# The soft-disc layer of a four-layer kernel: the disc projection with its columns as weights, one chain an image, and a new timetable

## The chip, the cores and the metric

The kernel runs on one core of one Trainium2 chip. A core has a matrix engine (TensorE, PE in the profile, with its weight loads shown apart as PEld), a vector engine (VectorE, DVE), an activation engine (ScalarE, ACT), a general engine (GpSimd, POOL) and a queue engine that issues the DMAs (SyncE, SP). Each works through its own list of instructions in order. The matrix engine writes to PSUM, of which this layer uses eight banks, and POOL works on SBUF only. The metric is device time in microseconds: the median of the runs.

## The reference, cut to what matters

Eight images of 32 x 32 tokens with 256 channels go through four layers, each of the form x + layer(groupnorm(x)). The change is in the fourth: attention in 8 heads of 32 over a 7 x 7 window, with a soft disc per token and head that masks the window.

```python
qkv = silu(x @ w_qkv.T);  q, k, v = split(qkv)
q = rope(rms_norm(q, w_qn));  k = rope(rms_norm(k, w_kn))   # over the 32 of a head
wp = silu(x @ w_wp.T + b_wp)                  # 16 columns: a width and a sharpness for each head
width = sigmoid(wp[..., :8]) * max_dist + 0.5
sharp = sigmoid(wp[..., 8:]) * 9.5 + 0.5
soft_mask = sigmoid((width - rel_dist) * sharp)
scores = scores - (1 - soft_mask) * 10000
out = softmax(scores) @ v_window
y = silu((rms_norm(out, w_on) + v) @ w_out.T)
```


Rope turns q and k of one head by the same angles, so it falls out of their product, and the kernel leaves it out. All arithmetic is in float32.

## The kernel before, in words

`layer3` (L2090) goes over 64 groups: 8 images, in each 2 chunks of 4 heads (a chunk J is image J // 2, half J % 2), in each chunk 4 column strips of the image. One group's life is spread over several turns of the main loop over m (the `for m in range(-2, N + 2)` in the printed code). In turn m the loop writes out, in this order, for all engines: the scores of group m + 2 (L1807, PE), the division of group m by its sums (L1843 on DVE, L1846 on POOL), the window mask of group m + 3 (L2241, POOL), the first four exponentials of group m + 1 (L1836, ACT), two of the four logits steps of group m + 2 (L1825, DVE), then fillers, the second four exponentials, the other logits, the turning of group m - 1 (L1858 transposes on PE, L1863 copies on DVE) in two halves, each half followed by fillers and by four tanh of group m + 4 (`soft`, L2234, ACT), then the product with the values of group m - 2 (L1873 PE, L1879 DVE). The order on PE, ACT, DVE and POOL is exactly the order written.

Everything else is a filler with a due time in turns and quarters of a turn: `fill.add(at, unit)`. `units(at)` issues those that are due, at four places in a turn: m after the first exponentials, m + 0.25 after the first half of the turning, m + 0.5 after the second half, m + 0.75 at the end. A unit's PE part, and for a projection also its ACT part, is issued at that place; what follows on DVE and POOL is a closure, and `finish()` runs one step of every open closure, four times a turn: before the fillers of m, after the second exponentials, and after each group of four `soft`.

The fillers of a chunk J, whose first group is n = 4J (`plan_chunk`, L2355): `project(J, s, h)` (L2146), two matmuls of 128 x 512 on the normed image xq, a tanh on ACT (L2143), then on DVE the product (L2168 for q, L2170 for k and v) and on POOL the square (L2178); s is 0 for q, 1 for k, 2 for v, h is the half of the image. `squares_sum` (L2245) sums the squares on PE, `roots` (L2267) takes their roots on ACT with a table load each way, `head_scales` (L2278) spreads them on PE and multiplies k and then q on DVE (L2288); the scores of the chunk wait for that product. `vturn` (L2292) and `keep` (L2298) write v to memory for the windows.

The fillers of an image b, n = 8b (`plan_image`, L2368): statistics, mean and root of the group norm, `normed(b, c)` (L2119, one ACT instruction of 1.23 us for each half of the channels, L418), the disc projection, and the tail of the image before (scale, output projection, store). `discs(b, u)` (L2184) takes four blocks of 128 tokens: for each block and each half of the channels the tokens are the weights and the 16 columns of w_wp, padded to 128, are streamed (L2191). The result lies with tokens on partitions. Then a chain of a bias add on DVE (L2198), tanh on ACT (L2206), a product on DVE (L2211), tanh on ACT (L2216), and three small DVE steps (`scales`, L2223 to L2225). There are two such chains an image. `soft` of the image's first group, in turn n - 4, reads the result.

Big tiles (an image, a normed image, the weights of the layer) come from a pool of three buffers (`K.big`, L168): the weights keep one for the whole layer, so x of an image and xq of an image take the other two, and xq of image b goes where xq of image b - 1 lay. PSUM tiles come from one ring of eight (`st.ring`, L1786).

Of the kernel before, what the change touches and what calls it, by code (L numbers as in the profile page):

```python
# [10 lines left out]
F32 = mybir.dt.float32  # L11
AF = mybir.ActivationFunctionType
ALU = mybir.AluOpType
# [3 lines left out]
P = 128  # L17
# [2072 lines left out]
def layer3(tc, K, src, dst, n_img, a, first):  # L2090
    nc = tc.nc
    with tc.tile_pool(name="l3c", bufs=1, reuse_waits="tile") as cp, tc.tile_pool(
        name="l3w", bufs=1, reuse_waits="tile"
    ) as wk, tc.tile_pool(name="l3p", bufs=1, space=PSUM, reuse_waits="tile") as pp:
        x, xq, vT, disc, xr, fac, sqs, tok = ({} for _ in range(8))

        def load(b):
            x[b] = K.big("x")
# [6 lines left out]
        st = DiscStream(K, wk, cp, pp, n_img, 6)  # L2105
# [40 lines left out]
        def project(J, s, h):  # L2146
            b, c = divmod(J, 2)
            if h == 0:
                if s == 0:
                    st.q[b, c] = wk.tile([P, L], F32, name="qT", bufs=2)  # L2150
                elif s == 1:
                    st.k[b, c] = kpad[J % 2]
                else:
                    vT[b, c] = wk.tile([P, L], F32, name="vT", bufs=5)
            ps = st.ring("qkv_ps")
            for kc in range(2):
                o = s * C + c * P
                nc.tensor.matmul(  # L2158
                    ps, w[:, kc, o : o + P], xq[b][:, kc, h * HALF : (h + 1) * HALF],
                    start=kc == 0, stop=kc == 1,  # L2160
                )
            th = half_silu(ps)

            def rest():
                d = dest(J, s, h)
                if s == 0:
                    q = st.q[b, c][:, h * HALF : (h + 1) * HALF]
                    nc.vector.scalar_tensor_tensor(q, th, 1.0, ps, ALU.add, ALU.mult)  # L2168
                for k in range(2 if s else 0):
                    nc.vector.scalar_tensor_tensor(  # L2170
                        d[:, k], part(th)[:, k], 1.0, part(ps)[:, k], ALU.add, ALU.mult
                    )
                if s == 2:
# [4 lines left out]
                nc.gpsimd.tensor_mul(part(sq), d, d)  # L2178

            return rest  # L2180

        def discs(b, u):  # L2184
            if u == 0:
                disc[b] = wk.tile([P, 8, 16], F32, name="disc", bufs=2)
            ps = st.ring("wp_ps")
            for i in range(4):
                tok = slice((4 * u + i) * P, (4 * u + i + 1) * P)
                for kc in range(2):  # L2190
                    nc.tensor.matmul(  # L2191
                        ps[:, i * P : (i + 1) * P], xq[b][:, kc, tok], w[:, kc, 768:],
                        start=kc == 0, stop=kc == 1,
                    )

            def rest():
                d = disc[b][:, 4 * u : 4 * u + 4, :]
                nc.vector.tensor_add(  # L2198
                    d, ps.rearrange("p (t g) -> p t g", g=P)[:, :, 0:16],
                    bwp.unsqueeze(1).to_broadcast([P, 4, 16]),  # L2200
                )
                return silu

            def silu():
                th = wk.tile([P, 4, 16], F32, name="dth", bufs=2)
                nc.scalar.activation(th, disc[b][:, 4 * u : 4 * u + 4, :], AF.Tanh)  # L2206
                return lambda: silu2(th)

            def silu2(th):
                d = disc[b][:, 4 * u : 4 * u + 4, :]  # L2210
                nc.vector.scalar_tensor_tensor(d, th, 1.0, d, ALU.add, ALU.mult)  # L2211
                return sigmoid

            def sigmoid():
                d = disc[b][:, 4 * u : 4 * u + 4, :]
                nc.scalar.activation(d, d, AF.Tanh, scale=0.5)  # L2216
                return scales

            def scales():
                d = disc[b][:, 4 * u : 4 * u + 4, :]  # L2220
                wd, sp = d[:, :, 0:8], d[:, :, 8:16]
                md = math.sqrt(2.0) * 3
                nc.vector.tensor_scalar(wd, wd, md / 2, md / 2 + 0.5, ALU.mult, ALU.add)  # L2223
                nc.vector.tensor_scalar(sp, sp, 9.5 / 4, 10.5 / 4, ALU.mult, ALU.add)
                nc.vector.scalar_tensor_tensor(wd, wd, -1.0, sp, ALU.mult, ALU.mult)  # L2225

            return rest

# [49 lines left out]
        def head_scales(J, s):  # L2278

            ps = [st.ring("fac_ps") for _ in range(2)]  # L2280
            for h in range(2):
                g = slice(32 * (2 * s + h), 32 * (2 * s + h) + 32)
                nc.tensor.matmul(ps[h], spread[g, s], fac[J][g], start=True, stop=True)

            def rest():
                for h in range(2):
                    d = dest(J, s, h)
                    nc.vector.tensor_mul(d, d, part(ps[h]))  # L2288

            return rest  # L2290
# [62 lines left out]
        fill = Fillers()  # L2353

        def plan_chunk(J):  # L2355

            n = 4 * J
            for i, at in enumerate((-6.75, -6.25, -5.75, -5.25)):
                fill.add(n + at, lambda i=i: project(J, 1 - i // 2, i % 2))
            for h in range(2):  # L2360
                fill.add(n - 5 + h / 4, lambda h=h: project(J, 2, h))
                fill.add(n - 4 + h / 4, lambda h=h: vturn(J, h))
                fill.add(n - 3 + h / 2, lambda h=h: head_scales(J, 1 - h))
            fill.add(n - 3.5, lambda: keep(J))

        def plan_image(b):
            n = 8 * b
            if b:  # L2368
                fill.add(n - 15, lambda: load(b))
                for i in range(4):  # L2370
                    fill.add(
                        n - 13 + i / 2 if b > 1 else -1.5 + i / 4,
                        lambda i=i: gn.stats(b, image_parts(x[b]), i),
                    )
                fill.add(max(n - 10, -0.5), lambda: gn.mean(b, later))
                fill.add(max(n - 9.5, 0.25), lambda: gn.root(b, later))
                for c in range(2):
                    fill.add(n - 8.5 + c if b > 1 else 0.75 + c / 4, lambda c=c: normed(b, c))
                for u in range(2):
                    fill.add(n - 6 + u / 2, lambda u=u: discs(b, u))  # L2380
            for c in range(2):
                fill.add(n + 6.75 + 3.5 * c, lambda c=c: tail_sq(b, c))
            fill.add(n + 12.75, lambda: tail_scale(2 * b + 4, b))


            for i in range(4):
                h, m = divmod(i, 2)
                fill.add(n + (14.5, 15, 15.25, 15.75)[i], lambda h=h, m=m: reload(b, m, h))
                fill.add(n + (15.5, 16.25, 16.5, 16.75)[i], lambda h=h, m=m: output(b, m, h))
# [155 lines left out]
```

## Time and profile before

| | |
|---|---|
| median of 3 runs | 3099.14 us (3091.14 to 3104.78) |
| the profiled execution | 3098.01 us |
| its span, first to last instruction | 3096.2 us |
| mean granted TensorE clock | 0.979 |
| the fourth layer | from about 2374 us (first L2191) to the end, some 720 us |
| one image in the steady part | 81.9 us (the same tanh of L2143 at 2611.78 and at 2693.69) |
| busy in 2600 to 2650 | PE 47.87, ACT 45.19, DVE 46.42, POOL 40.60 of 50 us |
| busy in 2650 to 2700 | PE 47.73, ACT 46.51, DVE 38.93, POOL 46.81 of 50 us |
| L2191, the disc projection on PE | 128 matmuls in the layer, 275 ns each as modelled (each recorded as two) |
| L2158, the other projections on PE | 192 matmuls, 592 ns each as modelled |

A line of the timeline has the start in us, the duration, the engine, the line, the operation with output and inputs, the count of merged instructions, and in brackets how long the engine stood idle before it and who released it. A matmul in float32 is recorded as two passes, so "x4" of L2158 are two matmuls. Matmuls are pipelined, so what a run of them costs is read from the start of one line to the start of the next, not from the durations.

### The profile page before, as it was taken

To read this page: it belongs to the slowest core of one execution; us is meant where nothing else is said; L and a number is where in the kernel's file an instruction comes from. 1 tells how busy PE (TensorE), PEld (TensorE's weight loads), DVE (VectorE), ACT (ScalarE), POOL (GpSimd) and SP (SyncE) were. 2 spreads that over 40 slices of the span, in tenths; PEclk is the share of its full clock that TensorE was granted. 3 is DMA by queue.
4 is the path that set the end of the run, shared out by engine and by line. 5 is a ranking of instruction groups with operands and counts; after the bars stand their busy time and mean duration, and the time that the engine had idled before them with its cause. 6 is when DMAs were issued, how large, how long until landed. Compare 5 with 4: busy or idle time off the path is not lost. (4 is left out here: it accounts for less than half of the span.)

```text
span 3096.2 us, 74829 instructions
## 1 busy us (share of the span) xinstructions
PE 2944.2 (95%) x29224; PEld 1573.7 (51%) x29224; DVE 2172.7 (70%) x5249; ACT 2136.7 (69%) x4833; POOL 1736.8 (56%) x1132
## 2 busy tenths in 40 slices
PE   7999999999999899999999999899998899999997
PEld 3323233232332344477777775666665455555554
DVE  4777777777778567766666665667675688888885
ACT  3667676676677556665555553677676899999994
POOL 4666666666666211144455444434344578888886
PEclk9999999999999999999999999999999899999997
DMA  3000000000001366789888864343443112222221
GB/s 140 12 28 1 28 18 11 28 1 28 21 8 42 105 236 233 262 222 225 216 199 216 213 180 162 103 134 106 137 122 117 52 56 83 82 85 82 70 71 61
DMA packets 246945, 325.07 MB, mean 105 GB/s; under 512 B 16192, under 2 KB 185216, under 8 KB 238272
## 3 DMA queue, kind: packets, MB, share of 16 engines
q1 hardware_dynamic: 240208, 299.92, 32.3%
q10 hardware_dynamic: 6384, 20.37, 1.9%
q8 instruction: 231, 3.78, 0.5%
q14 instruction: 122, 1.00, 0.1%
HBM read 216.70 MB, written 103.53 MB: 103 GB/s over the span
## 5 line engine op out<-in xcount | busy, mean ns | idle before, releaser
L693 DVE TENSOR_TENSOR e<-s,ret 128x1024 f32<-128x1024 f32 x512 | 602.4, 1218 | 175.0 <-PE s L687 172.5
L700 ACT ACTIVATE ea<-e 128x1024 f32<-128x1024 f32 x512 | 535.4, 1055 | 257.1 <-DVE e L693 234.5
L702 POOL TENSOR_TENSOR ea<-ea 128x1024 f32<-128x1024 f32 x128 | 304.0, 2375 | 285.7 <-ACT ea L700 217.7
L687 PE MATMUL s<-qk,qk 32*128 32x512 f32 x2048 | 302.2, 641 | 3.1 <-DVE e L693 1.3
L1705 POOL TENSOR_TENSOR e<-e,su 128x616 f32<-128x616 f32 (+2 forms) x128 | 156.6, 1229 | 263.4 <-DVE su L1704 237.4
L739 PE MATMUL num<-e,v 128*32 128x512 f32 x2048 | 271.3, 595 | 0.0
L1846 POOL TENSOR_TENSOR e<-e,su 128x784 f32<-128x784 f32 x128 | 188.8, 1497 | 84.0 <-DVE su L1843 79.8
L2234 ACT ACTIVATE e<-win,disc 128x196 f32<-128x196 f32 x512 | 235.4, 541 | 0.1
L869 PE MATMUL up_ps<-x,wup 128*128 128x512 f32 x512 | 229.1, 602 | 4.0 <-POOL x L237 3.2
L1836 ACT ACTIVATE e<-e,mx 128x196 f32<-128x196 f32 x512 | 226.8, 449 | 4.2 <-DVE mx L1825 4.2
L1700 ACT ACTIVATE e<-e,mx 128x154 f32<-128x154 f32 (+2 forms) x512 | 211.6, 420 | 4.6 <-DVE mx L1688 4.6
L712 PE MATMUL sm<-ea,ones 128*32 128x512 f32 x1536 | 209.6, 607 | 1.6 <-POOL ea L702 1.6
L1291 POOL TENSOR_TENSOR decayed<-state,rb 128x520 f32<-128x520 f32 x48 | 50.8, 1057 | 274.6 <-DVE state L1321 137.4
L1825 DVE CUSTOM_DVE_ANT_0 e<-s,e 128x196 f32<-128x196 f32 x512 | 153.1, 356 | 73.1 <-PE s L1807 63.1
L896 DVE SCALAR_TENSOR_TENSOR cv<-xm,par,cv 128x512 f32<-128x512 f32 x192 | 144.7, 754 | 80.6 <-ACT cv L891 75.9
L2158 PE MATMUL qkv_ps<-xq,w 128*128 128x512 f32 x384 | 192.0, 627 | 8.1 <-ACT xq L418 6.3
L2241 POOL TENSOR_TENSOR e<-e,win 128x784 f32<-128x784 f32 x128 | 198.8, 1575 | 0.3 <-ACT e L2234 0.3
L687 PEld LDWEIGHTS s<-qk,qk 32*128 32x128 f32 x2048 | 84.6, 183 | 195.6 <-issue 86.8
L1085 ACT ACTIVATE d<-d,cols 128x128 f32<-128x128 f32 x512 | 163.3, 391 | 14.3 <-POOL d L1076 13.7
L1863 DVE COPY pts<-pt 112x512 f32<-112x512 f32 x256 | 163.8, 683 | 1.5 <-PE pt L1858 1.5
L869 PEld LDWEIGHTS up_ps<-x,wup 128*128 128x128 f32 x512 | 95.5, 191 | 117.7 <-issue 106.5
L1076 POOL TENSOR_TENSOR d<-cmask,d 128x1024 f32<-128x1024 f32 x64 | 154.0, 2408 | 0.0
(236 smaller groups left out, 6466.9 us busy)
## 6 DMA issues: line engine op xcount, KB each, us to landing
d<-l1rows SPq DMA_DIRECT2D x64, 512.0 KB
x<-x SPq DMA_DIRECT2D x25, 1024.0 KB
v<-l3v SPq DMA_DIRECT2D x320, 56.0 KB
l1xm<-xm SPq DMA_DIRECT2D x16, 1024.0 KB
l1sz<-sz SPq DMA_DIRECT2D x16, 1024.0 KB
xv<-l1xm SPq DMA_DIRECT2D x32, 512.0 KB
l1xa<-xa SPq DMA_DIRECT2D x16, 1024.0 KB
xa<-l1xa SPq DMA_DIRECT2D x16, 1024.0 KB
```

Source lines behind the costliest of these rows:

```text
L687: nc.tensor.matmul(s[:, j % 2], qk[b, 1, c][g, kb * P : (kb + 1) * P], qk[b, 0, c][g, h * HALF : (h + 1) * HALF], start=True, stop=True,)
L693: nc.vector.tensor_mul(e[n, i], s, m)
L700: nc.scalar.activation(ea[n, i], e[n, i], AF.Abs)
L702: nc.gpsimd.tensor_add(ea[n, i], ea[n, i], ea.pop((n - 1, i)))
L712: nc.tensor.matmul(acc["sm"][g, :], ones, two[j // 2][:, j % 2, :], start=kb == 0 and k == 0, stop=kb == 4 and k == 2,)
L739: nc.tensor.matmul(acc["num"][g, :], v[b][:, kb, vc], e[n, j // 2][:, j % 2, :], start=kb == 0, stop=kb == 7,)
L869: nc.tensor.matmul(ps, wup[:, kc, m * P : (m + 1) * P], seg(s)[:, kc], start=kc == 0, stop=kc == 1,)
L1700: self.nc.scalar.activation(p[:, j], p[:, j], AF.Exp, scale=-1.0, bias=mx[:, i, j : j + 1], accum_out=su[:, j : j + 1],)
L1836: self.nc.scalar.activation(e[:, j], e[:, j], AF.Exp, scale=-1.0, bias=mx[:, g, j : j + 1], accum_out=su[:, g, j : j + 1],)
L2158: nc.tensor.matmul(ps, w[:, kc, o : o + P], xq[b][:, kc, h * HALF : (h + 1) * HALF], start=kc == 0, stop=kc == 1,)
L2234: nc.scalar.activation(e[:, j], win[:, 0], AF.Tanh, scale=disc[b][:, i, 8 + h : 9 + h], bias=disc[b][:, i, h : h + 1],)
L2241: nc.gpsimd.tensor_add(e, e, win[:, 1].unsqueeze(1).to_broadcast([P, 4, NWIN]))
```

## The change

The disc projection is turned round: 32 columns of the weights (16 real, 16 zero) are the weights of four tiles of the matrix engine, 32 columns wide each, and each tile streams a quarter of the image (256 tokens). All four results lie in one PSUM bank, 32 partitions each. DVE copies that bank to SBUF, two transposes turn it back to tokens on partitions, and from there one chain of the same kind runs for the whole image instead of two for half each. The last three steps of the chain (`scales`) go from DVE to POOL. The due times change: the first projection of k and both of q are a quarter of a turn earlier, `head_scales` of k is a quarter later, the root of the group norm a quarter earlier, `normed` half a turn and three quarters earlier, and the disc projection sits at -5.75 and -5.5 instead of -6 and -5.5. In `start()` the disc projection comes alone first, and its turning between the two projections of k.

```diff
-        def discs(b, u):
-            if u == 0:
-                disc[b] = wk.tile([P, 8, 16], F32, name="disc", bufs=2)
+        def discs(b):
             ps = st.ring("wp_ps")
-            for i in range(4):
-                tok = slice((4 * u + i) * P, (4 * u + i + 1) * P)
-                for kc in range(2):
+            for kc in range(2):
+                for i in range(4):
                     nc.tensor.matmul(
-                        ps[:, i * P : (i + 1) * P], xq[b][:, kc, tok], w[:, kc, 768:],
-                        start=kc == 0, stop=kc == 1,
+                        ps[32 * i : 32 * i + 32, 0:256], w[:, kc, 768:800],
+                        xq[b][:, kc, 256 * i : 256 * i + 256],
+                        start=kc == 0, stop=kc == 1, skip_group_check=True,
                     )
             def rest():
+                turned[b] = wk.tile([P, 256], F32, name="dsb")
+                nc.vector.tensor_copy(turned[b], ps[:, 0:256])
+            return rest
+
+        def disc_turns(b):
+            d = disc[b] = wk.tile([P, 8, 16], F32, name="disc", bufs=2)
+            t, ps = turned.pop(b), st.ring("dt")
+            for i in range(2):
+                nc.tensor.transpose(
+                    ps[:, i * P : i * P + P], t[:, i * P : i * P + P], K.ident
+                )
+            def rest():
                 nc.vector.tensor_add(
-                    d, ps.rearrange("p (t g) -> p t g", g=P)[:, :, 0:16],
-                    bwp.unsqueeze(1).to_broadcast([P, 4, 16]),
+                    d.rearrange("p (q t) g -> p t q g", t=2),
+                    ps[:, 0:256].rearrange("p (t q g) -> p t q g", t=2, g=32)[:, :, :, 0:16],
+                    bwp.unsqueeze(1).unsqueeze(1).to_broadcast([P, 2, 4, 16]),
                 )
                 return silu
...
             def scales():
-                nc.vector.tensor_scalar(wd, wd, md / 2, md / 2 + 0.5, ALU.mult, ALU.add)
-                nc.vector.tensor_scalar(sp, sp, 9.5 / 4, 10.5 / 4, ALU.mult, ALU.add)
-                nc.vector.scalar_tensor_tensor(wd, wd, -1.0, sp, ALU.mult, ALU.mult)
+                nc.gpsimd.tensor_scalar(wd, wd, -md / 2, -md / 2 - 0.5, ALU.mult, ALU.add)
+                nc.gpsimd.tensor_scalar(sp, sp, 9.5 / 4, 10.5 / 4, ALU.mult, ALU.add)
+                nc.gpsimd.tensor_mul(wd, wd, sp)
...
-            for i, at in enumerate((-6.75, -6.25, -5.75, -5.25)):
+            for i, at in enumerate((-7, -6.25, -6, -5.5)):
                 fill.add(n + at, lambda i=i: project(J, 1 - i // 2, i % 2))
...
-                fill.add(n - 3 + h / 2, lambda h=h: head_scales(J, 1 - h))
+                fill.add(n - 2.75 + h / 4, lambda h=h: head_scales(J, 1 - h))
...
-                fill.add(max(n - 9.5, 0.25), lambda: gn.root(b, later))
+                fill.add(max(n - 9.75, 0), lambda: gn.root(b, later))
                 for c in range(2):
-                    fill.add(n - 8.5 + c if b > 1 else 0.75 + c / 4, lambda c=c: normed(b, c))
-                for u in range(2):
-                    fill.add(n - 6 + u / 2, lambda u=u: discs(b, u))
+                    fill.add(n - 9 + 0.75 * c if b > 1 else 0.25 + c / 4, lambda c=c: normed(b, c))
+                fill.add(n - 5.75, lambda: discs(b))
+                fill.add(n - 5.5, lambda: disc_turns(b))
...
-            rest = [discs(0, 0), discs(0, 1), project(0, 1, 0)]
-            all_of(rest[0], rest[2])
-            all_of(rest[1], project(0, 1, 1))
+            all_of(discs(0))
+            rest = [project(0, 1, 0), disc_turns(0), project(0, 1, 1)]
+            all_of(*rest)
```

The tanh steps of the chain now work on 128 elements a partition instead of 64, and `d` is the whole tile `disc[b]`.

More of the change, by code (lines that the diff above doesn't have):

```diff
@@ L2094, in layer3 @@
     ) as wk, tc.tile_pool(name="l3p", bufs=1, space=PSUM, reuse_waits="tile") as pp:
-        x, xq, vT, disc, xr, fac, sqs, tok = ({} for _ in range(8))
+        x, xq, vT, disc, xr, fac, sqs, tok, turned = ({} for _ in range(9))
         def load(b):
@@ L2180, in project @@
             return rest
-        def discs(b, u):
-            if u == 0:
-                disc[b] = wk.tile([P, 8, 16], F32, name="disc", bufs=2)
+        def discs(b):
             ps = st.ring("wp_ps")
-            for i in range(4):
-                tok = slice((4 * u + i) * P, (4 * u + i + 1) * P)
-                for kc in range(2):
+            for kc in range(2):
+                for i in range(4):
                     nc.tensor.matmul(
-                        ps[:, i * P : (i + 1) * P], xq[b][:, kc, tok], w[:, kc, 768:],
-                        start=kc == 0, stop=kc == 1,
+                        ps[32 * i : 32 * i + 32, 0:256], w[:, kc, 768:800],
+                        xq[b][:, kc, 256 * i : 256 * i + 256],
+                        start=kc == 0, stop=kc == 1, skip_group_check=True,
                     )
             def rest():
-                d = disc[b][:, 4 * u : 4 * u + 4, :]
+                turned[b] = wk.tile([P, 256], F32, name="dsb")
[9 more added lines that the diff above has]
+            def rest():
                 nc.vector.tensor_add(
-                    d, ps.rearrange("p (t g) -> p t g", g=P)[:, :, 0:16],
-                    bwp.unsqueeze(1).to_broadcast([P, 4, 16]),
+                    d.rearrange("p (q t) g -> p t q g", t=2),
+                    ps[:, 0:256].rearrange("p (t q g) -> p t q g", t=2, g=32)[:, :, :, 0:16],
+                    bwp.unsqueeze(1).unsqueeze(1).to_broadcast([P, 2, 4, 16]),
                 )
@@ L2204, in silu @@
             def silu():
-                th = wk.tile([P, 4, 16], F32, name="dth", bufs=2)
-                nc.scalar.activation(th, disc[b][:, 4 * u : 4 * u + 4, :], AF.Tanh)
+                th = wk.tile([P, 8, 16], F32, name="dth", bufs=2)
+                nc.scalar.activation(th, d, AF.Tanh)
                 return lambda: silu2(th)
             def silu2(th):
-                d = disc[b][:, 4 * u : 4 * u + 4, :]
                 nc.vector.scalar_tensor_tensor(d, th, 1.0, d, ALU.add, ALU.mult)
@@ L2214, in sigmoid @@
             def sigmoid():
-                d = disc[b][:, 4 * u : 4 * u + 4, :]
                 nc.scalar.activation(d, d, AF.Tanh, scale=0.5)
@@ L2219, in scales @@
             def scales():
-                d = disc[b][:, 4 * u : 4 * u + 4, :]
                 wd, sp = d[:, :, 0:8], d[:, :, 8:16]
                 md = math.sqrt(2.0) * 3
-                nc.vector.tensor_scalar(wd, wd, md / 2, md / 2 + 0.5, ALU.mult, ALU.add)
-                nc.vector.tensor_scalar(sp, sp, 9.5 / 4, 10.5 / 4, ALU.mult, ALU.add)
-                nc.vector.scalar_tensor_tensor(wd, wd, -1.0, sp, ALU.mult, ALU.mult)
+                nc.gpsimd.tensor_scalar(wd, wd, -md / 2, -md / 2 - 0.5, ALU.mult, ALU.add)
+                nc.gpsimd.tensor_scalar(sp, sp, 9.5 / 4, 10.5 / 4, ALU.mult, ALU.add)
+                nc.gpsimd.tensor_mul(wd, wd, sp)
             return rest
```

## The prediction

> **What bounds the kernel now.** The change is in the last layer alone, so I read that stretch and no share of the whole span: first the busy time of each engine in stretches of 50 us, then the waits of each engine from 2450 to 3000 us, then the order of time around one disc projection.
>
> The stretches (PE, PEld, DVE, ACT, POOL, granted clock, DMA share, GB/s):
>
> ```profile
> 2600.00:2650.00 50.00, 47.87 (x547) 29.43 (x546) 46.42 (x153) 45.19 (x141) 40.60 (x30) 1.00 0.29 87
> 2650.00:2700.00 50.00, 47.73 (x539) 28.96 (x537) 38.93 (x136) 46.51 (x132) 46.81 (x36) 1.00 0.33 101
> ```
>
> No engine stands out, so waits decide. ACT's, from 2450 to 3000 us:
>
> ```profile
> ACT th L2143 <- PE qkv_ps L2158: 34.2, 42, 3.9
> ACT th L2143 <- PE out_ps L2333: 1.6, 7, 0.2
> ACT th L2143 <- POOL e L2241: 1.6, 2, 0.8
> ACT xq L418 <- DVE gn L231: 0.9, 1, 0.9
> ```
>
> That is its whole list: outside it ACT works without a pause. So ACT sets the pace, and time is lost only where a projection's tanh stands for PE. In the image from 2611.78 to 2693.69 (81.9 us) these stands are 1.30, 1.32 and 0.23 in the even chunk and 0.73, 1.02, 0.38, 0.18 and 0.23 (the last for L2333) in the odd one: 2.85 and 2.54, together 5.39 us. The first two lie at the disc projections, as the timeline shows:
>
> ```profile
> 2606.18 0.93 PE L1807 MATMUL s<-kp,qT 32*64 32x196 f32 x32
> 2607.04 2.05 PE L2191 MATMUL wp_ps<-w,xq 128*128 128x128 f32 x16
> 2609.80 1.88 PE L2158 MATMUL qkv_ps<-xq,w 128*128 128x512 f32 x4
> 2611.78 0.60 ACT L2143 ACTIVATE th<-qkv_ps 128x512 f32<-128x512 f32 x1 [1.30 <-PE qkv_ps L2158]
> 2612.39 1.95 PE L2191 MATMUL wp_ps<-w,xq 128*128 128x128 f32 x16
> 2615.29 1.98 PE L2158 MATMUL qkv_ps<-xq,w 128*128 128x512 f32 x4
> 2617.37 0.60 ACT L2143 ACTIVATE th<-qkv_ps 128x512 f32<-128x512 f32 x1 [1.32 <-PE qkv_ps L2158]
> ```
>
> Each disc block holds PE 1.9 us (2607.04 to 2608.93), and after each the tanh of q is late.
>
> **PE, part by part.** Removed: two blocks of 1.88, 3.76 us an image. Added: eight matmuls of 256 columns on 32-column tiles. The nearest row is `squares_sum`, L2253: four matmuls of 512 in four such tiles start at 2707.36 and the next line at 2708.22, 0.86 us. Ours have the same columns for each tile, so 0.86. Going into and out of narrow tiles costs something: L1873's 448 columns a tile would last 448 x 1.68 ns = 0.75 (1.68 from L2253's 0.86 / 512), and it takes 1.02 from start to start, so 0.27. The two transposes: four of L1888 take 0.49 (2710.93 to 2711.42), so 0.25. Sum 1.38; PE gains 2.4 us an image (bounds 2.1 if the transposes pay 0.27 too, 2.65 if tiles switch free).
>
> The Trainium skill, "TensorEngine Tiling (Array Packing)", section Key Properties, speaks against this: a change of tiling mode drains the engine. It gives no duration, and the new order puts one narrow stint between full-width transposes that had none; by the rule the cost is one drain in and one out, which the trace's 0.27 for L1873 would already hold.
>
> **ACT.** Four small tanh become two of twice the width. In place such a tanh takes 0.15 (2614.04 to the `soft` at 2614.19); two of up to 0.21 leave a gain of 0.17 an image (bounds 0.1 and 0.3).
>
> **DVE and POOL of the chain.** DVE loses ten steps an image and gets a copy (0.41, L1879's row), an add (0.22 to 0.41) and one product (0.22 alone, 1.96 at worst in L2211's row, when POOL works on SBUF): 40.7 us over 15 chains become about 10. DVE is not waited for there, since ACT waits for PE only, so I cost it at nothing. POOL's three steps of 64 elements: from 1.04 (512 elements) and 1.50 (784) the slope is 1.7 ns an element and the rest 0.17, so 0.27 each; L224's 0.71 for two elements is the other end; 0.8 to 2.1 in all. The cover is POOL's wait here, with `soft` of the next image on ACT only at 2634.52:
>
> ```profile
> 2622.60 1.03 POOL L2178 TENSOR_TENSOR sq<-qT 128x512 f32<-128x512 f32 x1
> 2630.48 2.95 POOL L1846 TENSOR_TENSOR e<-e,su 128x784 f32<-128x784 f32 x2 [6.84 <-DVE su L1843]
> ```
>
> Without that cover they would cost ACT up to 2.1 us an image.
>
> **The new due times, even chunk.** Here a gain is given back. k's first tanh moves ahead of four exponentials (0.44 each from start to start): ACT is free of the tanh of 2598.34 at 2598.82, does four exponentials, reaches it at 2600.6 and ends at 2601.1, and DVE, whose next closure is its product, stands from 2599.6 (before, it scaled k there). DVE is full from there on: product 0.66, logits 1.13, copies 1.2, k scale 1.2, copies 1.2, q scale 1.2 end at 2607.7 instead of 2606.13. The scores wait for the q scale, so they end at 2608.56 and q's first projection (1.72 + 0.15 to its tanh) at 2610.4. ACT comes at 2608.9 (four exponentials, eight `soft` of 0.46, k's second tanh of 0.5 and four exponentials after 2601.1) and stands 1.6 us where it stood 1.30. Then PE is early: turning 0.87, discs 1.13, turning 0.87, q's second half 1.72 end at 2615.0, ACT comes at 2614.7 and stands 0.25 instead of 1.32; v's second wait of 0.23 goes. Stands 1.85 instead of 2.85, a gain of 1.0 (bounds: 2.85 if q's scale is not late, minus 0.5 if DVE slips another 1.5).
>
> **Odd chunk.** The same move without a disc projection taken out. k's first tanh no longer stands (PE's part is done at 2638.9, ACT comes at 2639.8), its second stands 0.7 instead of 1.02: ACT, earlier by the lost wait and the tanh it has done, comes at 2645.8, and PE, which needs a PSUM bank that DVE's second copy of the turning frees, has it ready at 2646.5. But q's scale ends at 2648.15 as before, the scores at 2648.55, and q's first projection at 2650.6, while ACT, now coming before its four exponentials, is there at 2648.8: 1.85 us where it had none. New too: `normed` moves to n - 9, between the v projections of the image before, whose xq lies in the buffer that it writes. It must wait for the second v projection, a half turning (0.87) and a projection (1.72) behind the first on PE: about 1.0 us, and behind it stand four exponentials, whose sums POOL divides. The waits of 0.38, 0.18 and 0.23 go. Sum 0.7 + 1.85 + 1.0 = 3.55 against 2.54: a loss of 1.0 (bounds: gain 0.5, loss 2.5). Elsewhere: PE waits up to 3.4 us, 19.3 us in seven places, for the square of q before `squares_sum`; q's second half now comes earlier and POOL squares it ahead of the division. That goes, but ACT has no wait behind it, so it is worth nothing. `head_scales` of k moves one `finish` later on DVE; q's, for which the scores wait, stays.
>
> **The start.** Image 0: the first tanh of L2143 (2379.94) comes 2.7 us sooner, but the first `soft` waits for the chain, which now ends on POOL behind memsets that last to 2381.35, two squares (2.1) and its own 0.8 to 2.1: 2384.3 to 2385.6 against 2384.07; I take 0.5 us lost. Image 1: PE waits for xq.
>
> ```profile
> 2433.36 2.08 PE L2158 MATMUL qkv_ps<-xq,w 128*128 128x512 f32 x2 [5.53 <-ACT xq L418]
> 2438.37 0.60 ACT L2143 ACTIVATE th<-qkv_ps 128x512 f32<-128x512 f32 x1 [0.40 <-PE qkv_ps L2158]
> 2445.68 0.60 ACT L2143 ACTIVATE th<-qkv_ps 128x512 f32<-128x512 f32 x1 [3.19 <-PE qkv_ps L2158]
> ```
>
> `normed` moves from 0.75 and 1.0 to 0.25 and 0.5, so xq is complete 3.5 us sooner, and the stands of 0.40 and 3.19 go: 3.6 (bounds 0 and 3.6). Together 3.1 gained.
>
> **Sum.** Seven even chunks at -1.0, seven odd at +1.0, seven times -0.17, start -3.1: -4.3 us. The profiled execution took 3098.0 (span 3096.2 and 1.8 around it), so 3093.7; the median of the runs lies 1.1 above it. I predict 3094, with a range of its own of 3086 to 3103.
>
> **Rivals.** *PE's time arrives in full.* If q's scale is not late, and q's tanh finds its projection ready, seven images save the even chunk's 2.85 + 0.17 and the odd one stays as it was: 21 us, with the start 24, 3074. For it: the two largest stands are at the blocks that shrink. Against: PE waits for DVE's scale at 2606.18, and making the block behind it shorter doesn't move that. *The tanh ahead of the exponentials holds ACT.* At both chunks' first q projection ACT now comes 1.77 us (four exponentials) sooner than PE can serve it. If DVE's q scale slips by 1.5 us more than I have, each of 14 places costs 1.5 more: 21 us, 3115. It turns the gain into a loss from 0.3 us a place on (4.3 / 14), and makes the kernel slower by over 0.5% from 1.5. For it: DVE was full before both places, and its small steps last up to 1.6 us beside POOL. Against: its PSUM-reading copies and scales keep their 0.68 all through. *The change doesn't do what it says:* the four tiles run one after the other, 3.4 instead of 0.86, q's second tanh is 2.6 late again: 7 x 2.3 more, 3110. L2253's row speaks against it.
>
> **How the numbers follow.** What a measurement of this kernel can tell from no change is about 0.5%, 15.5 us. Forecast 0.60, PE's time in full 0.24, ACT held 0.12, tiles in sequence 0.04 (within 0.5% as well). So faster 0.24, same 0.64, slower 0.12. The range takes most of both rivals: 3075 to 3112.
>
> **What would show it.** L2191 gone, eight matmuls in about 0.9 us and a stint of about 1.1 to the next line; ACT's stands at 1.6 and 0.25 in the even chunk, 0.7 and 1.85 in the odd one, and L418 standing about 1.0 for PE; no wait of L2253 for POOL; the 3.19 at the start gone; an image of 81.7 us. Wrong would be: ACT waiting for POOL at the first `soft` of an image, or an image below 80.5 or above 83.

## The result, and the profile after

The changed kernel takes 3115.59 us (median of 12 runs, 3111.74 to 3120.15); beside it the kernel before took 3102.19 us (12 runs). The ratio is 1.0046, with a 95% interval of 1.0034 to 1.0058: the change costs some 14 us. The prediction was 3094, and its range ended at 3112. The profiled execution after took 3111.74 us, with a span of 3109.7 us, and its mean granted clock is 0.973 (before 3096.2 and 0.979).

The time went into the steady part of the fourth layer. From the division of the first image's first group (L1843 on DVE) to that of the last image's it is 575.1 us before and 593.2 after, so 2.6 us an image are lost in the mean, and 3.3 in an undisturbed one (85.2 against 81.9).

In the changed kernel's lines L2188 is the disc projection, L2204 its turning, L2222 the product of its chain, L2226 the second tanh of its chain, L2232 to L2234 its scales on POOL, L2243 `soft`, L2262 `squares_sum`, L2283 `roots`, L2292 and L2297 the two halves of `head_scales` (PE, DVE), L2331 the scale of the tail, L2349 the product behind the output projection. L2143, L2158, L2170, L418, L1807, L1836, L1858 and L1873 are as before.

The stretches of 50 us after (PE, PEld, DVE, ACT, POOL, granted clock, DMA share, GB/s):

```profile
2600.00:2650.00 50.00, 44.85 (x518) 25.81 (x522) 44.70 (x146) 47.95 (x143) 43.02 (x34) 0.99 0.27 81
2650.00:2700.00 50.00, 47.40 (x483) 26.48 (x474) 35.87 (x129) 42.82 (x123) 41.37 (x31) 0.94 0.32 99
```

ACT's waits after, from 2450 to 3000 us (us in total, times, longest); this is the whole list:

```profile
ACT th L2143 <- PE qkv_ps L2158: 49.7, 33, 4.1
ACT xq L418 <- PE qkv_ps L2158: 10.3, 6, 1.7
```

The first line was 34.2 before, in 42 places; now it is fewer places and longer ones. The second line is new. So the frame of the prediction holds: ACT still sets the pace and loses time only to late projections. What is new on the other engines is who waits for k. DVE's and then PE's waits after, in the same stretch:

```profile
DVE kp L2170 <- ACT th L2143: 23.2, 13, 5.9
```

```profile
PE pt L1858 <- DVE kp L2170: 20.4, 13, 5.5
```

Before, the second was not there, and the first was short:

```profile
DVE kp L2170 <- ACT th L2143: 3.8, 2, 3.2
```

Around one such place, an odd chunk's turn n - 7, the timeline of the changed kernel reads:

```profile
2724.61 1.98 PE L2158 MATMUL qkv_ps<-xq,w 128*128 128x512 f32 x4
...
2729.23 0.57 ACT L2143 ACTIVATE th<-qkv_ps 128x512 f32<-128x512 f32 x1
2729.83 0.75 DVE L2170 SCALAR_TENSOR_TENSOR kp<-th,qkv_ps 128x256 f32<-128x256 f32 x2 [0.89 <-ACT th L2143]
2730.73 0.78 PE L1858 MATMUL pt<-idg,e 128*112 128x128 f32 x4 [1.08 <-DVE kp L2170]
2731.44 2.46 PE L2292 MATMUL fac_ps<-fac,spread 32*128 32x512 f32 x4
2732.83 1.28 DVE L2297 TENSOR_TENSOR kp<-kp,fac_ps 128x512 f32<-128x512 f32 x2
2733.83 1.94 PE L1873 MATMUL o<-pts,v 112*32 112x128 f32 x40
2735.70 3.05 PE L2158 MATMUL qkv_ps<-xq,w 128*128 128x512 f32 x4
2738.79 0.60 ACT L2143 ACTIVATE th<-qkv_ps 128x512 f32<-128x512 f32 x1 [3.69 <-PE qkv_ps L2158]
```

k's first projection is done on PE early, but ACT comes to its tanh only behind four exponentials. DVE's next step is the product of that tanh, so DVE stands 0.89 us; PE's transposes write to PSUM alone, and the last four of the turn stand 1.08 us. They go on 0.15 us behind the end of that product (2729.83 and 0.75), as in all 13 places, and 2.1 us ahead of the scale of k (L2297, 2732.83). Now the durations: the spreading for q takes 2.46 us where that for k, at 2727.40, takes 1.41, the values 1.94 instead of 1.09, and k's second projection 3.05 instead of 1.98. The granted clock (the column behind POOL) in windows of 4 us says why:

```profile
2726.00:2730.00 4.00, 3.46 (x18) 1.91 (x16) 3.11 (x9) 4.00 (x14) 4.00 (x4) 1.00 0.33 96
2730.00:2734.00 4.00, 3.27 (x12) 1.47 (x16) 4.00 (x14) 4.00 (x14) 4.00 (x4) 0.63 0.04 11
2734.00:2738.00 4.00, 4.00 (x43) 2.60 (x40) 2.94 (x7) 1.10 (x3) 4.00 (x4) 0.51 0.05 16
```

PE works at half speed for about 7 us after the pause (3.4 us of clock are lost in the last two windows), and ACT, with 1.10 us of work in the last window, waits for it. I read the clock of every run from 2450 to 3000 us in windows of 2 us, counted the stretches of windows below 0.9, and added up (1 - clock) x 2 us: before 5 stretches and 10.2 us, after 12 stretches and 34.1 us.

### The profile page after: what moved, and what is told of

The parts are those of the page before. It is cut to its first block, busy times and chain, and to the rows that moved or that the text cites. A ratio compares the mean times of both kernels' runs of the same rounds, so it can differ in the third digit from the quotient of the medians.

```text
span 3109.7 us, 74566 instructions
## 1 busy us (share of the span) xinstructions
PE 2941.5 (95%) x29112; PEld 1555.5 (50%) x29112; DVE 2150.6 (69%) x5193; ACT 2132.5 (69%) x4817; POOL 1743.7 (56%) x1156
## 3 DMA queue, kind: packets, MB, share of 16 engines
q8 instruction: 231, 3.78, 0.5%
## 5 line engine op out<-in xcount | busy, mean ns | idle before, releaser
L2243 ACT ACTIVATE e<-win,disc 128x196 f32<-128x196 f32 x512 | 236.1, 541 | 2.9 <-POOL disc L2234 2.8
L1836 ACT ACTIVATE e<-e,mx 128x196 f32<-128x196 f32 x512 | 226.9, 448 | 4.2 <-DVE mx L1825 4.2
L2158 PE MATMUL qkv_ps<-xq,w 128*128 128x512 f32 x384 | 204.1, 660 | 5.8 <-ACT xq L418 5.3
L1858 PE MATMUL pt<-idg,e 128*112 128x128 f32 x1024 | 142.1, 281 | 31.1 <-DVE kp L2170 20.4
L1858 PEld LDWEIGHTS pt<-idg,e 128*112 128x112 f32 x1024 | 117.5, 138 | 86.0 <-issue 44.3
```

The lines of the kernel that those rows point to most:

```text
L1836: self.nc.scalar.activation(e[:, j], e[:, j], AF.Exp, scale=-1.0, bias=mx[:, g, j : j + 1], accum_out=su[:, g, j : j + 1],)
L1858: self.nc.tensor.transpose(d[:, g, k], self.tile(n)[:, g, j, k * self.PART : (k + 1) * self.PART], self.K.ident,)
L2158: nc.tensor.matmul(ps, w[:, kc, o : o + P], xq[b][:, kc, h * HALF : (h + 1) * HALF], start=kc == 0, stop=kc == 1,)
L2243: nc.scalar.activation(e[:, j], win[:, 0], AF.Tanh, scale=disc[b][:, i, 8 + h : 9 + h], bias=disc[b][:, i, h : h + 1],)
```

## The experiments

Each kernel was compared with the kernel before on the same chip; ratios carry a 95% interval. Two theories stood at the start: that the new place of k's `head_scales`, on DVE behind k's first product, is the loss (with the fallen clock as what carries it, or with the waits alone), and that `normed`, which now waits for its buffer, is.

**The two halves of the change.** The disc form with all old due times (against the changed kernel):

```diff
-            for i, at in enumerate((-7, -6.25, -6, -5.5)):
+            for i, at in enumerate((-6.75, -6.25, -5.75, -5.25)):
-                fill.add(n - 2.75 + h / 4, lambda h=h: head_scales(J, 1 - h))
+                fill.add(n - 3 + h / 2, lambda h=h: head_scales(J, 1 - h))
-                fill.add(max(n - 9.75, 0), lambda: gn.root(b, later))
+                fill.add(max(n - 9.5, 0.25), lambda: gn.root(b, later))
-                    fill.add(n - 9 + 0.75 * c if b > 1 else 0.25 + c / 4, lambda c=c: normed(b, c))
+                    fill.add(n - 8.5 + c if b > 1 else 0.75 + c / 4, lambda c=c: normed(b, c))
```

> The new form of the disc projection with all due times of the chunks and of the group norm as they were before (the projection at -5.75, its turning at -5.5). Theory 1, k's first projection a quarter earlier holds a PSUM bank in the turn where the scale of k now comes late, PE stands for banks, and its clock falls to half for k's second projection: none of that here, no half-speed k projection, ACT's stands at the q projections shrink to under 0.5 each; 8 to 20 us faster than before. Theory 2, the normalised image waits 1.72 us for its buffer, six times: also gone here, as fast as in theory 1. Theory 3, the disc chain itself costs (its three steps on POOL, the copy, the tiles): as slow as the changed kernel, about 3115.

Measured: 3082.1 us, ratio 0.9949 (0.993 to 0.9967). And the same four lines the other way round, the old disc projection with the new due times:

> The old disc projection, both halves at -6 and -5.5, with the new due times of the chunks and of the group norm. Theory 1 (banks and half clock in the turn of k's first projection): slower than the changed kernel's 1.0046, because the 2.4 us of PE an image are not saved either: 1.006 to 1.012 of before, with k's second projection at half speed in most chunks. Theory 3 (the disc chain costs): within 0.2% of before.

Measured: 3124.99 us, ratio 1.0078 (1.006 to 1.0096). So the disc form gains some 16 us by itself, and the timetable is the whole loss. ACT's list for the old form at the new times has the same 49.7 and 10.3 as the changed kernel's, and 2.3 more. The path is not the same, though: there PE waits for kp 7.2 us in 3 places only, and the clock loses 20.5 us in 10 stretches. What the new times cost the old form besides was not followed.

**Which due time.** First the times of the chunk put back and those of the norm left new (the first two pairs of the diff above):

> The changed kernel with the due times of projections and head scales as before, and the group norm's new ones kept. Theory 1: ACT's stands at k's second projection (2.5 and 3.7 us) go, but L418 still stands about 1.7 for the buffer six times: 5 to 10 us slower than the disc form with all old times, 0 to 12 us faster than before. Theory 2 (the buffer wait alone made the change slower): still 10 us slower than before.

Measured: 3102.92 us, 1.0009 (0.9997 to 1.0021). Against the disc form alone only the norm's times differ, so these cost 0.6% in that company. Then the reverse, `normed` alone put back for the images after the second:

```diff
-                    fill.add(n - 9 + 0.75 * c if b > 1 else 0.25 + c / 4, lambda c=c: normed(b, c))
+                    fill.add(n - 8.5 + c if b > 1 else 0.25 + c / 4, lambda c=c: normed(b, c))
```

> The changed kernel with normed back at -8.5 and -7.5 for images 2 to 7. Theory 2 (buffer wait): 10 us faster than the changed kernel, that is about as before, 3102 to 3106. Theory 1 (banks and half clock): the wait of L418 goes but the stands at k's second projection stay at 2.5 to 3.7; gains at most 1.7 x 6 = 10 us, less where the time turns up at the next stand for PE: 3105 to 3112.

Measured: 3119.54 us, 1.0063 (1.0044 to 1.0083). The 10.3 us of L418 are gone from ACT's list, and yet nothing is gained: the stands at L2158 rise to 53.9, and the clock falls in 15 stretches. The wait for the buffer by itself is not the cause.

**PE kept busy, first attempt.** The spreading matmuls of `head_scales` issued three times:

```diff
-                nc.tensor.matmul(ps[h], spread[g, s], fac[J][g], start=True, stop=True)
+                for _ in range(3 if J else 1):
+                    nc.tensor.matmul(ps[h], spread[g, s], fac[J][g], start=True, stop=True)
```

> The changed kernel with each matmul of head_scales issued three times into the same PSUM bank (the same result, some 3.4 us more work for PE a chunk, placed where PE stands for banks). Theory 1a, half of ACT's stand at k's second projection is the clock, which falls to half because PE pauses in the turn before: the k projection runs at 1.7 instead of 3.0 us, the stands of 2.5 to 3.9 us shrink by about 2 at some 14 places, and the kernel with more work is 10 to 25 us faster than the changed one, 3090 to 3106. Theory 1b, only the waits for banks count and the clock follows from the delay: no gain, or up to 10 us slower than the changed kernel, 3115 to 3125.

Measured: 3177.17 us, 1.0233 (1.02 to 1.0267). PE's wait for kp fell from 20.4 to 4.2 us, but ACT's stands rose to 91.7: the added matmuls stand ahead of k's second projection and of the scales themselves, so they lengthen the path. Inconclusive on the clock, which still fell in 9 stretches.

**k's scale, and its order against k's first projection.** Only `head_scales` put back:

```diff
-                fill.add(n - 2.75 + h / 4, lambda h=h: head_scales(J, 1 - h))
+                fill.add(n - 3 + h / 2, lambda h=h: head_scales(J, 1 - h))
```

> The changed kernel with head_scales back at -3 and -2.5 alone; k's first projection stays at -7, so that both fall into one place, the scale first. Theory 1 (DVE stands for k's first tanh with the scale of k behind it): DVE scales k before it stands, the banks come free sooner, the stands at k's second projection shrink below 2 in the even chunk; 5 to 15 us faster than the changed kernel. If the place of head_scales is without effect: 3115.

Measured (e6 below): 3089.96 us, 0.9958 (0.9945 to 0.9971), and PE's wait for kp at the turning is gone. This one quarter of a turn is worth 0.9%, some 27 us, for q's `head_scales` is at -2.5 in both. Only k's first projection put back, which then follows k's `head_scales` at the same place:

```diff
-            for i, at in enumerate((-7, -6.25, -6, -5.5)):
+            for i, at in enumerate((-6.75, -6.25, -6, -5.5)):
```

> The changed kernel with k's first projection back at -6.75 alone, head_scales of k at the same place ahead of it. Theory 1 (k's first projection is what starts the stands): no half-speed k projection, stands at k's second projection under 1; with the buffer wait of L418 still there 3100 to 3106, near the run with all chunk times back. Rival (q's tanh ahead of the exponentials is what costs): stays at about 3115.

Measured: 3097.37 us, 0.9981 (0.997 to 0.9991): a little below the 3100 to 3106 of Theory 1, and not the rival's 3115. Then the order alone, against the kernel of the scale put back:

```diff
-            for i, at in enumerate((-7, -6.25, -6, -5.5)):
+            for i, at in enumerate((-7.01, -6.25, -6, -5.5)):
```

> The kernel of e6 (k's `head_scales` at -3, ratio 0.9958), with the first projection of k a hundredth of a turn sooner: both are issued at the same place of the turn as there, but the projection comes first, so that its product stands ahead of the scale of k on DVE. Nothing else differs. Theory 1 (the scale stands on DVE behind a product that waits for ACT's tanh, and holds its PSUM banks as long): most of the loss of the changed kernel comes back, 3105 to 3118 (ratio 1.000 to 1.006), with PE waiting for banks in the turning and k's second projection late for ACT. Rival (what costs is only that `head_scales` is issued a quarter of a turn later): as e6, 3085 to 3095.

Measured (e10 below): 3110.49 us, 1.0022 (1.0009 to 1.0034). Both units are issued at the same place of the turn, and swapping them brings back 20 of the 27 us, with the wait:

```profile
PE pt L1858 <- DVE kp L2170: 20.0, 12, 6.0
```

So most of the loss is the order of the two units and not the quarter of a turn. The time is that of Theory 1; its reason, that the scale standing behind the product holds PE, is not what the trace shows. The place from above reads in this run:

```profile
2729.73 0.76 DVE L2170 SCALAR_TENSOR_TENSOR kp<-th,qkv_ps 128x256 f32<-128x256 f32 x2 [0.89 <-ACT th L2143]
2730.40 1.28 DVE L2297 TENSOR_TENSOR kp<-kp,fac_ps 128x512 f32<-128x512 f32 x2
2730.63 0.62 PE L1858 MATMUL pt<-idg,e 128*112 128x128 f32 x4 [1.09 <-DVE kp L2170]
```

PE goes on behind the product, when the scale has only begun. In the kernel with the scale first, all the transposes of that turn run without a wait, and most of them before the product starts:

```profile
2720.15 2.20 PE L1858 MATMUL pt<-idg,e 128*112 128x128 f32 x16
2722.16 0.74 DVE L2170 SCALAR_TENSOR_TENSOR kp<-th,qkv_ps 128x256 f32<-128x256 f32 x2
```

So the order decides whether the transposes wait for k's product at all. It may decide which unit's PSUM bank comes round to them; no run reads the banks, so that is not shown. Next the changed kernel with k's first projection sooner still, so that its tanh is done when DVE comes:

```diff
-            for i, at in enumerate((-7, -6.25, -6, -5.5)):
+            for i, at in enumerate((-7.25, -6.25, -6, -5.5)):
```

> The changed kernel with the first projection of k a quarter of a turn sooner still, at -7.25, ahead of the divisions and of the first four exponentials; k's `head_scales` stays late at -2.75. Theory 1 (DVE's queue: the product of k stands for its tanh and the scale of k behind it): the tanh is done before DVE's product comes, the scale is not held, the banks come free; ratio near e6's, 0.994 to 0.999, and PE's wait for kp at the turning (24 us in 550) falls under 8. Rival (a late `head_scales` costs by itself, since PE's spreading matmuls and the scale then fall into the turning whatever stands ahead of them): 1.002 to 1.007.

Measured (e11 below): 3116.7 us, 1.0047 (1.0031 to 1.0063). Half a miss: PE's wait for kp fell from 20.4 to 5.4 us, as expected, and the time stayed, as did ACT's stands (58.1 us in all, 60.0 in the changed kernel). Its windows around ACT's longest stand (6.64 us, ending at 2662.80) show what took its place:

```profile
2648.00:2652.00 4.00, 3.34 (x45) 2.01 (x44) 3.75 (x17) 4.00 (x17) 2.63 (x2) 1.00 0.31 87
2652.00:2656.00 4.00, 3.82 (x12) 2.03 (x12) 4.00 (x14) 4.00 (x12) 4.00 (x4) 0.53 0.20 57
2656.00:2660.00 4.00, 4.00 (x45) 2.10 (x42) 4.00 (x8) 0.15 (x1) 4.00 (x4) 0.50 0.00 0
```

Two pauses of 0.31 and 0.35 us in the turning, and the clock is at half for the next 8 us all the same. It fell in 10 stretches here, three of them at a wait that is new: PE stands 4.1 us for the second tanh of the disc chain (L2226). That asked for a test of the clock that leaves the path alone.

**The pause filled.** The changed kernel with the four transposes ahead of PE's wait written three times into the same bank, which DVE reads only after that wait; 14 places:

```diff
-        for g in range(2):
+        for _ in range(3 if j == 2 and n % 4 == 0 and n < 56 else 1):
+            for g in range(2):
```

> The changed kernel, with the four transposes ahead of PE's wait for the product of k (L1858, the second half of the turning in the turn of k's first projection) written three times into the same bank: eight transposes more, about 0.87 us of work, in a place where PE stands 0.95 to 1.08 us for a bank anyway, and where DVE reads the result only after that wait. 14 places. The waits, the order and all due times stay. Theory C (the granted clock falls to half because of this pause, and the half clock makes the second projection of k late): PE's wait there shrinks to 0.1 to 0.3, the clock stays at 1.00 in most of those places (12 stretches below 0.9 between 2450 and 3000 us become 3 to 6), the second projection of k takes 1.9 to 2.0 instead of 2.9 to 3.1, ACT's stands for L2158 fall from 49.7 to 25 to 38, and the kernel takes 3093 to 3107. Rival (the wait for the bank is the whole cost and the clock only follows): stands and time as in the changed kernel, 3112 to 3122. Second rival (other pauses take the clock down as well, as in e5): the clock's stretches stay at 9 to 12 and the time within 6 us of the changed kernel.

Measured: 3099.64 us, 1.0003 (0.9989 to 1.0017): 112 transposes whose results nobody needs make the changed kernel 0.4% faster. The same place in its timeline (all lines behind L1853 are one higher here):

```profile
2728.89 1.52 PE L1859 MATMUL pt<-idg,e 128*112 128x128 f32 x12 [0.20 <-DVE oT L2332]
2730.62 0.62 PE L1859 MATMUL pt<-idg,e 128*112 128x128 f32 x4 [0.21 <-DVE kp L2171]
2731.18 1.65 PE L2293 MATMUL fac_ps<-fac,spread 32*128 32x512 f32 x4
2732.77 1.09 PE L1874 MATMUL o<-pts,v 112*32 112x128 f32 x40
2733.78 1.98 PE L2159 MATMUL qkv_ps<-xq,w 128*128 128x512 f32 x4
...
2735.81 0.60 ACT L2144 ACTIVATE th<-qkv_ps 128x512 f32<-128x512 f32 x1 [0.81 <-PE qkv_ps L2159]
```

and its windows:

```profile
2726.00:2730.00 4.00, 3.80 (x24) 2.50 (x23) 3.11 (x7) 4.00 (x15) 4.00 (x4) 1.00 0.32 88
2730.00:2734.00 4.00, 3.79 (x53) 2.30 (x52) 4.00 (x15) 4.00 (x14) 4.00 (x4) 1.00 0.06 18
2734.00:2738.00 4.00, 3.93 (x39) 1.71 (x39) 3.89 (x13) 3.19 (x12) 4.00 (x4) 1.00 0.18 54
```

DVE's wait for the tanh is as long as ever (23.1 us in all), and PE's transposes go on at the same moment (6.12 us behind the start of k's first projection in both), but the clock stays at 1.00 and ACT's stand shrinks from 3.69 to 0.81 us. At this place the wait itself costs little, and the half clock behind it 2.9 us. Over the whole kernel, filling the pauses gives back 0.43%, about half of the 0.88% that putting `head_scales` back gives; what the other half is was not separated. In the even chunks the clock still falls (4 of the 6 stretches left), behind another pause, of 1.43 us, that was not filled.

**Towards a better kernel.** The disc form with the old due times, and its projection a quarter of a turn sooner:

```diff
-                fill.add(n - 5.75, lambda: discs(b))
+                fill.add(n - 6, lambda: discs(b))
```

> The disc form with all old times, and the disc matmuls at -6 instead of -5.75, so that the turning does not stand for DVE's copy (0.84 us of PE an image in the run before). ACT's stand of 1.4 at q's second projection shrinks to 0.3 to 0.8, its stand at q's first grows by at most 0.4: 0 to 6 us faster than with -5.75, 3076 to 3083.

Measured: 3089.59 us, 0.9957 (0.9944 to 0.997), no better than at -5.75 and above the 3076 to 3083 expected. Last, the changed kernel with both `head_scales` and, for the images after the second, `normed` put back; k's first projection, those of q and the root stay early:

```diff
-                fill.add(n - 2.75 + h / 4, lambda h=h: head_scales(J, 1 - h))
+                fill.add(n - 3 + h / 2, lambda h=h: head_scales(J, 1 - h))
-                    fill.add(n - 9 + 0.75 * c if b > 1 else 0.25 + c / 4, lambda c=c: normed(b, c))
+                    fill.add(n - 8.5 + c if b > 1 else 0.25 + c / 4, lambda c=c: normed(b, c))
```

> The changed kernel with two due times back as before: `head_scales` at -3 and -2.5, and `normed` at n - 8.5 and n - 7.5 for images after the second. The disc form, the first projection of k at -7, those of q at -6 and -5.5 and the root at n - 9.75 stay. Theory 1 (the move of k's `head_scales` behind k's first projection is the loss, and `normed` waiting for its buffer, 1.72 us in six places, is a second and smaller one): ACT's 10.3 us at L418 go, and they arrive, so about 3080 where e6 took 3090 (ratio 0.992 to 0.995). Theory 2 (that wait only takes the place of another, as it did when `normed` alone was put back with k's `head_scales` late): the 10.3 us turn up at a projection of k, and the ratio stays at 0.995 to 0.997.

Measured: 3065.75 us (3062.91 to 3072.01), 0.9888 (0.9867 to 0.9908): faster than both kernels, by 1.1% and 1.6%, and by more than either theory had. ACT's waits from 2450 to 3000 us:

```profile
ACT th L2143 <- PE qkv_ps L2158: 10.3, 22, 1.3
ACT xq L418 <- DVE gn L231: 2.3, 6, 1.0
ACT th L2143 <- PE out_ps L2342: 0.7, 4, 0.2
...
```

An image takes 77.7 us. Putting `normed` back is worth 0.7% here and was worth nothing while k's scale was late. What it removes beside L418's stand is seen in the kernel with the scale alone put back. There, in each even chunk, PE pauses for the product behind the output projection, and the clock falls again; its timeline:

```profile
2757.87 1.51 PE L1807 MATMUL s<-kp,qT 32*64 32x196 f32 x28 [1.43 <-DVE th L2349]
2759.31 2.87 PE L2292 MATMUL fac_ps<-fac,spread 32*128 32x512 f32 x4
2762.11 3.78 PE L2158 MATMUL qkv_ps<-xq,w 128*128 128x512 f32 x4
...
2765.99 0.60 ACT L2143 ACTIVATE th<-qkv_ps 128x512 f32<-128x512 f32 x1 [2.65 <-PE qkv_ps L2158]
```

With `normed` at its old places this wait is no longer in PE's list, the clock falls in 3 stretches instead of 8, and the 2.65 is gone. While k's scale is late there is a pause in the turning of every chunk, and the clock falls with or without that one.

## Why the prediction was wrong, by its own steps

**ACT as the bound, and stands as the measure**: right. The image from L418 at 2751.96 to L418 at 2837.20 has stands of 2.51, 0.42 and 0.48 in the even chunk, 3.78, 0.42 and 1.72 in the odd one: 9.33 us against 5.39, so 3.9 more, where the image is 3.3 longer. At 85.2 us it is above the 83 named as a sign of being wrong.

**The step that failed** is what was made of DVE's stand for k's first tanh. I had seen that DVE would stand there ("before, it scaled k there") and passed the delay on to q's scale alone; I let `head_scales` of k move "one `finish` later on DVE" at no cost, because the scores wait for q's, and of the disc chain I had said "DVE is not waited for there". The stand goes to PE: the transposes of the same turn wait for k's product (20.4 us in 13 places), and k's second projection is behind them. I had 0.7 us for k's second stand in the odd chunk and none in the even one; measured are 3.78 and 2.51. The order of k's scale and k's first projection is worth 20 us (e10 against e6), and it turned a gain into a loss; why the transposes wait for the product in one order and not in the other stays open. Behind that lies a second omission: the sums for the two chunks used PE's durations at full clock. At the place shown, most of the stand (2.9 of 3.69 us) is the half clock after the pause, as the filled pause shows.

**The rivals.** "The tanh ahead of the exponentials holds ACT" came nearest in its figure (3115), but that was luck, for its mechanism is not what happened: the early tanh does hold an engine, but DVE first and then PE, at k and not at q; its price at q did not come (q's first stands are 0.42, not 1.85 and 1.6). "PE's time in full" came nearer than the forecast for the disc form by itself: 3082.1 for that form, against 3074 and 3094. (The forecast's own sum gives 3094.8 as the median, 3093.7 and 1.1.) "The tiles run in sequence" is refuted below.

**The disc projection and the start.** The timeline of the changed kernel:

```profile
2383.59 1.87 ACT L2243 ACTIVATE e<-win,disc 128x196 f32<-128x196 f32 x4 [2.82 <-POOL disc L2234]
...
2441.59 3.34 PE L2158 MATMUL qkv_ps<-xq,w 128*128 128x512 f32 x4
2444.96 0.60 ACT L2143 ACTIVATE th<-qkv_ps 128x512 f32<-128x512 f32 x1 [3.73 <-PE qkv_ps L2158]
...
2786.72 1.07 PE L2188 MATMUL wp_ps<-xq,w 128*32 128x256 f32 x16
2787.72 1.08 PE L1858 MATMUL pt<-idg,e 128*112 128x128 f32 x8
```

The eight matmuls take 1.00 us from start to start; 0.86 + 0.27 had been reckoned, so the price was right, and the four tiles do run side by side. The three steps on POOL take 0.24, 0.24 and 0.32 us (0.27 each reckoned), and in the steady part nobody waits for them. The product on DVE (L2222) takes 1.6 us in the median, near the upper end given, and ACT stands 0.8 us for it once, at the start. The first `soft` does wait for POOL, but little of the 0.5 us is lost: it comes 9.71 us behind the start of the first disc matmul (2373.88), before 9.62 us (2374.45). And the 3.19 us at image 1 were not won: xq comes 1.4 us sooner (its projection starts at 2431.97 instead of 2433.36), yet k's second projection takes 3.34 us at half clock (3.67 before), and the stand is 3.73.

**q, `squares_sum` and `normed`.** PE's wait for POOL at `squares_sum` went, as predicted (the 19.3 us are those of its weight loads; its matmuls waited 12.9 us in six places); no run shows that it was worth anything. L418 stands 1.72 us in six places for the second v projection, where 1.0 had been reckoned: a term mis-sized. The sums of the two chunks came to 3.41 instead of 1.85 (even) and 5.92 instead of 3.55 (odd): q's first stands, where I put the loss, are smaller than reckoned by 1.2 and 1.4 us, and k's second take more than that back.

**What is not settled.** How much of the 0.5% of the disc form is PE's time (two blocks of 1.88 us an image became 1.00 and two transposes) and how much the smaller chain was not separated. It was not found what makes up the half of the loss that filling the pauses leaves, nor why k's first projection at -7.25 leaves the turning with pauses that take the clock down.

## What to carry to other kernels

When a unit is moved by a quarter of a turn, list what it passes on each in-order engine: here a projection passed a scale, PE's transposes came to wait for a product that waits for ACT, and the wait travelled from DVE to PE and back to ACT. A new pause of PE may cost more than its own length: behind 12 of 13 such pauses here PE worked at half the clock for some 3 to 10 us. Before a schedule is judged, read the granted clock in windows of 2 to 4 us, since a mean of 0.97 hid it. Parts of a change should be timed apart: here the disc form gained 0.5%, one due time lost 0.9%, and with two due times put back the kernel is 1.1% faster than before.

## What the runs showed of the hardware that was not expected

In the changed kernel 12 of PE's 13 waits for kp, 0.95 to 5.51 us long, lie at a stretch in which the granted clock goes to 0.50: within some 2 us of the wait's end, or during the longest. The stretches last 4 to 12 us in windows of 2 us below 0.9, which is 3 to 10 us at half the clock by the clock lost in them. The length of one pause does not decide: two of 0.31 and 0.35 us were followed by half clock (e11), while six of 1.47 us (L1888 for ACT's roots) in the changed kernel were not. Nor does the place: the pause of 1.43 us for the product behind the output projection was followed by it in five of five places in e6, and in none of five in the changed kernel. The Trainium skill, "TensorE: Matmul & The Clock Gate", section "HAM oscillation — how this bites in real kernels", warns of idle gaps above about 3.4 us; here gaps of a third of that and less were enough in most places, so the measurement decides. Its section "A second HAM failure mode: psum-queue depth-cycling", on short idle times between groups of matmuls that make the clock go to and fro, agrees with these traces. What sets it off, in terms that one could plan by, no run here shows; that filling 14 pauses of a microsecond with dead transposes is worth 0.4% was measured.
